# Per-token adapter with LayerNorm on one core: start of the kernel reordered, additions of b2 moved from VectorE to GpSimd and TensorE

## The chip, the core and the metric

The kernel runs on one core of a Trainium2 chip. The core has five engines, each with its own instruction stream: TensorE (PE; its weight loads are listed as PEld), VectorE (DVE), ScalarE (ACT), GpSimd (POOL) and SyncE (SP, which here only issues DMAs). They meet through semaphores. The metric is device time in microseconds (us); lower is better. The profile gives, for one execution, the span from the first to the last instruction.

## The reference

Every batch entry b has 128 tokens of 512 values, and a language id that chooses one of 10 small adapters:

```
w1, w2 = W1[id], W2[id]                    # 512x128 and 128x512
h       = relu(x @ w1 + b1[id])
y       = x + h @ w2 + b2[id]
normed  = (y - mean(y)) * rsqrt(var(y) + 1e-5)
out     = x + normed * gamma[id] + beta[id]
```

x is 128 x 128 x 512 in float32, all weights are float32; b1, b2, gamma and beta are small random rows, ten of each. Everything is read from and written to HBM once: 43.85 MB read, 33.55 MB written.

## The kernel before, in words

One batch entry (128 tokens on the 128 partitions, 512 columns) is the unit of work, and "b" counts them, 0 to 127. x comes in groups of four entries (`load_x`, four buffers, pool `xp`), results go out in pairs (`store`, tile `o`, five buffers, pool `op`, so pair g uses the buffer of pair g-5 once that pair's store has landed). For each entry:

- PE transposes x in four blocks (`transpose_x`, L235), ACT copies the result from PSUM (`copy_xT`, L239), PE multiplies by w1 (`down`, L258), ACT applies bias and relu (`relu`, L266), PE multiplies by w2 into a PSUM tile `y` of a pool of five (`up`, L275). ACT also copies the chosen w1 out of a resident table (`stage_w1`, L226).
- b2 is added in one of three ways. By default POOL makes r = x + b2 ahead of time (`add_b2`, L245, tile `r`, four buffers) and the residual reads r in place of x. For entries chosen by `b2_by_vector`, DVE adds b2 to y in PSUM (`vector_b2`, L285). For those of `b2_by_matmul`, PE adds a one-row product to y (`up`, L274).
- DVE adds the residual and sums the rows (`residual`, L292), ACT squares and sums (`square`, L315) and takes a reciprocal root (L325), DVE refines it (L329 to L334), multiplies by gamma (`scale`, L358) and writes the result on top of o (`finish`, L367). o was filled beforehand by POOL with x + beta (`add_beta`, L252).

The order on every engine is the order of the text, held by `keep()`, which chains each instruction to the one before it on its engine. The loop variable is i; entry i is transposed, entry i-1 goes through `down`, entry i-2 through `up`, and b = i-3 through the residual. POOL is told to do `add_b2(b + 2)` and then `add_beta(b)`: r is made two entries ahead of the loop's b, o at b itself. That is an order, not a time: POOL starts each as soon as its inputs and its buffer are there.

All loads and nearly all stores go through the SP queue in the order of the text: x (0,1), w2 of three languages, w1 of single entries (`load_first`, L154), x in halves of a group (`load_part`, L89), the rest of w2, two halves of a table of w1 (`load_early`, L162), then inside the loop x groups (L71), stores (L371) and, at i = 8, 10, 12 and 14, four quarters of a second table of w1 (`load_w1`, L103).

At the start, the thirty rows of beta, gamma and b2 (tile `rows`) must be spread over all partitions. DVE cuts them into three bf16 parts (L184 to L188, tile `parts`), PE multiplies a selecting column by the parts (`spread`, L206) and ACT or DVE copies each row out of PSUM (L209, L211), beta first, then gamma, then b2. Before that, PE runs ten matmuls on constants (`spin`). The first four entries' transposes and `down`s are mixed into the spreads.

At the end (b from 123 on) POOL does, in its order: the last r, the last four additions of beta, then for entries 123 and 124 the multiplication by gamma and the addition to o (`by_pool`, L415 and L417), and a quarter of entry 125. ACT issues the stores of 124 and 125 (`store_last`, L420), SP those of 126 and 127.

Of the kernel before, what the change touches and what calls it, by code (L numbers as in the profile page):

```python
# [22 lines left out]
U = 2  # L23
# [3 lines left out]
def cond_resid_kernel(ctx: ExitStack, tc: tile.TileContext, x, itok, W1, b1, W2, b2, gamma, beta, out):  # L27
# [8 lines left out]
    nc = tc.nc  # L36
    B, S, H = x.shape
    L, _, A = W1.shape
# [28 lines left out]
    E = B - 5  # L67
# [6 lines left out]
    def xb(b):  # L74
        return xs[b // G][:, b % G, :]
# [3 lines left out]
    rows = rp.tile([P, H], FP, tag="r", name="rows")  # L79
# [7 lines left out]
    def load_part(lo, hi):  # L87
        dst = xs[lo // G][:, lo % G : lo % G + hi - lo, :]
        keep(nc.sync.dma_start(out=dst, in_=x[lo:hi].rearrange("b s h -> s b h")))  # L89

    keep(nc.sync.dma_start(out=ids, in_=itok.rearrange("(o b) -> o b", o=1)))
    keep(nc.scalar.dma_start(out=rows[0:L, :], in_=beta))
    keep(nc.sync.dma_start(out=rows[L : 2 * L, :], in_=gamma))
    keep(nc.scalar.dma_start(out=rows[2 * L : 3 * L, :], in_=b2))
    load_part(0, 2)
    keep(nc.scalar.dma_start(out=b1r, in_=b1))

    warm = const.tile([P, 1], FP, name="warm")
# [2 lines left out]
    def load_w1(k):  # L101
        keep(
            nc.sync.dma_start(out=w1[:, :, k, :], in_=W1[:, k * P : (k + 1) * P, :].rearrange("l p a -> p l a"))  # L103
        )

    ident = const.tile([P, P], FP, name="ident")
    make_identity(nc, ident)
    eps = const.tile([P, 1], FP, name="eps")
    nc.gpsimd.memset(eps, EPS)
    ones = const.tile([P, P], BF, name="ones")  # L110
    nc.gpsimd.memset(ones, 1.0)

    R = 3 * L
    parts = const.tile([P, H], BF, name="parts")
# [16 lines left out]
    def lid(b, engine):  # L133
        g = b // G
        if (g, engine) not in lids:
            loads, vals = nc.values_load_multi_w_load_instructions(  # L136
                lang[0:1, g * G : (g + 1) * G],
                engines=[engine],
                min_val=0,
                max_val=L - 1,  # L140
                skip_runtime_bounds_check_because="clamped on the chip to 0..L-1 above",
            )
            for ins in loads:
                keep(ins)
            lids[g, engine] = vals
        return lids[g, engine][b % G]
# [33 lines left out]
    load_early(5, L)  # L180
    load_part(2 * G + 2, 3 * G)

    left = rp.tile([P, H], FP, tag="r", name="left")
    keep(nc.vector.tensor_copy(parts[0:R, :], rows[0:R, :]))  # L184
    keep(nc.vector.tensor_tensor(left[32 : 32 + R, :], rows[0:R, :], parts[0:R, :], ALU.subtract))
    keep(nc.vector.tensor_copy(parts[32 : 32 + R, :], left[32 : 32 + R, :]))
    keep(nc.vector.tensor_tensor(left[64 : 64 + R, :], left[32 : 32 + R, :], parts[32 : 32 + R, :], ALU.subtract))
    keep(nc.vector.tensor_copy(parts[64 : 64 + R, :], left[64 : 64 + R, :]))  # L188

    b1T = const.tile([P, L], FP, name="b1T")  # L190

# [23 lines left out]


    def b2_by_matmul(b):
        return b in (5, B - 1)

    def b2_by_vector(b):  # L220
        return b < 4 or 8 <= b < B - 8 and (b % 4 == 1 if b < 24 else b % 16 in (1, 6, 11) or b % 32 == 30)

    def stage_w1(b):
        w1s[b] = wp.tile([P, KC, A], FP, tag="w1s", name=f"w1s_{b}")
# [12 lines left out]
    def copy_xT(b):  # L237
        xT[b] = tp.tile([P, KC, P], FP, tag="xT", name=f"xT_{b}")
        keep(nc.scalar.copy(xT[b], pxs.pop(b)))  # L239

    def add_b2(b):
        if not b2_by_matmul(b) and not b2_by_vector(b):
            rs[b] = rp.tile([P, H], FP, tag="r", name=f"r_{b}")
            v = lid(b, ET.Pool)
            keep(nc.gpsimd.tensor_tensor(rs[b], xb(b), b2_b[:, bass.ds(v * H, H)], ALU.add))  # L245

    def add_beta(b):
        g, j = divmod(b, 2)
        if j == 0:
            os[g] = op.tile([P, 2, H], FP, tag="o", name=f"o_{g}")  # L250
        v = lid(b, ET.Pool)
        keep(nc.gpsimd.tensor_tensor(os[g][:, j, :], xb(b), beta_b[:, bass.ds(v * H, H)], ALU.add))  # L252

    def down(b):
        phs[b] = p_h.tile([P, P], FP, tag="h", name=f"ph_{b}")
        for k in range(KC):
            keep(
                nc.tensor.matmul(  # L258
                    phs[b], lhsT=w1s[b][:, k, :], rhs=xT[b][:, k, :], start=(k == 0), stop=(k == KC - 1)
                )  # L260
            )
        del xT[b], w1s[b]
# [217 lines left out]
    def spin(n, width):  # L480
        idle = p_s.tile([P, H], FP, tag="s", name="idle")
        for _ in range(n):
            keep(
                nc.tensor.matmul(
                    idle[:, :width], lhsT=ones, rhs=ones[:, 0:1].to_broadcast([P, width]), start=True, stop=True
                )
            )


    spin(9, H)  # L490
    spin(1, H // 2)

    def spread_turn(lo, hi):
        for r in range(lo, hi):
            spread(r, nc.scalar if r % 7 in (1, 3, 5) else nc.vector)

    def x_turn(b):
        transpose_x(b)
        copy_xT(b)

    x_turn(0)
    transpose_b1()
    spread_turn(0, 4)
    x_turn(1)
    spread_turn(4, 11)
    down(0)
    relu(0)
    spread_turn(11, 15)
    down(1)
    relu(1)  # L510
    x_turn(2)
    spread_turn(15, 19)
    x_turn(3)
    down(2)
    relu(2)
    spread_turn(19, 24)
    down(3)
    relu(3)
    spread_turn(24, R)
    up(0)  # L520
    up(1)

    for i in range(3, B + U):
        b = i - U - 1
        if b > G and b % G == 2 and b // G + 3 < NG:
            load_x(b // G + 3)
        if i == 5:
            load_x(3)
        if i in (8, 10, 12, 14):
            load_w1((i - 8) // 2)  # L530
        if i == 4:
            up(2)
        if i == 5:
            up(3)
        if i > 3 and on(i):
            transpose_x(i)
        if b <= E:
            add_b2(b + 2)
            add_beta(b)
        if i > 4 and on(i - 1):  # L540
            down(i - 1)
        if i > 3 and on(i):
            copy_xT(i)
        if b == 2:
            scalar_means(0)
            deviation(0)
        if i > 4 and on(i - 1):
            relu(i - 1)
        if i + 1 >= LATE and on(i + 1):
            stage_w1(i + 1)  # L550
        if i > 5 and on(i - U):
            up(i - U)


        g, half = divmod(b, 2)
        p = g - 1
        mine, old = 0 <= p < B // 2, 0 <= p - 1 < B // 2
        if b == E:
            add_b2(b + 3)
            add_beta(b + 1)  # L560
            add_b2(b + 4)
            for n in range(b + 2, B):
                add_beta(n)
        if b > E:
            tail(b)
        elif half == 0:
            if on(b):
                vector_b2(b)
                residual(b)
                square(b)  # L570
            if mine:
                scale(2 * p)
                rstd(p, 1)
            if old:
                finish(2 * p - 1)
                store(p - 1)
        else:
            if on(b):
                vector_b2(b)
            if mine:  # L580
                rstd(p, 2)
            if on(b):
                residual(b)
                square(b)
            if mine:
                rstd(p, 3)
                scale(2 * p + 1)
            if mine:
                finish(2 * p)
        if 0 < g and b <= E and half == 1:  # L590
            scalar_means(g)
            deviation(g)
        if FIRST <= i + 1 < LATE:
            stage_w1(i + 1)

        for n, engine in ((i + 3, ET.Activation), (i - U + 3, ET.PE), (b + 1, ET.DVE), (b + 5, ET.Pool)):
            if on(n):
                lid(n, engine)

# [36 lines left out]
```

## Time and profile before

| what | value |
|---|---|
| time, median of 3 runs | 308.75 us (308.27 to 308.82) |
| span of the profiled execution | 306.5 us (the page gives no other time of it) |
| granted TensorE clock, mean | 0.989 |
| busy: PE / DVE / ACT / POOL | 294.6 / 295.9 / 282.3 / 283.9 us |
| `add_beta` (L252), `add_b2` (L245) on POOL | 128 and 97 instructions |
| `vector_b2` (L285) on DVE | 29 instructions, 695 ns each |
| moved by DMA | 77.85 MB |

How to read it: a row of the timeline is start, duration, engine, line, operation, tiles and count, and in brackets how long the engine was idle before it and what ended the idle time. Spans of POOL instructions overlap their neighbours, so the distance from one start to the next, not the duration, is what an instruction costs. In the list of waits the three numbers are the total, the count and the longest, in us. The windows table gives busy time per engine in a stretch, then the granted clock, the DMA engines' busy share and the rate in GB/s.

### The profile page before, as it was taken

Reading aid. Unit: us, or ns where it says so; the run is one execution under the profiler, and the core shown is the slowest. Engines: PE = TensorE matmul, PEld = TensorE weight load, DVE = VectorE, ACT = ScalarE, POOL = GpSimd, SP = SyncE. Lnnn points to the kernel's source line nnn. Section 1 sums busy time; section 2 is a strip of 40 time slices with the busy share of each in tenths; the row PEclk is TensorE's granted clock in tenths of the full one; section 3 lists DMA queues with packets and bytes.
Section 4 is the critical chain, followed back from the end, with each engine's and each line's share of the span. In section 5 each row is a group of like instructions: output and inputs, shape, how many; then the busy total and the mean of one; then the engine's idle time right before and its main releaser. Section 6 shows DMA issues by size and latency. Waiting matters only on the chain. (4 is left out here: it accounts for less than half of the span.)

```text
span 306.5 us, 6981 instructions
## 1 busy us (share of the span) xinstructions
PE 294.6 (96%) x1835; PEld 220.0 (72%) x1835; DVE 295.9 (97%) x771; ACT 282.3 (92%) x777; POOL 283.9 (93%) x238
## 2 busy tenths in 40 slices
PE   8999999999999999999999999999999999999960
PEld 3748787777777777777777777777777777777730
DVE  6889999999999999999999999999999999999985
ACT  3858999999999999999999999999999999999981
POOL 1349899999999999999999999999999999999994
PEclk9999999999999999999999999999999999999995
DMA  6999999976678766766777666767776666773324
GB/s 231 379 390 388 373 371 354 387 231 240 221 255 276 250 202 241 226 257 219 259 276 243 213 209 238 265 224 260 275 238 206 226 231 242 246 266 137 135 109 171
DMA packets 43769, 77.85 MB, mean 254 GB/s; under 512 B 1961, under 2 KB 7348, under 8 KB 43730
## 3 DMA queue, kind: packets, MB, share of 16 engines
q1 hardware_dynamic: 43382, 76.84, 72.1%
q10 hardware_dynamic: 348, 0.57, 0.5%
q8 instruction: 15, 0.25, 0.3%
q14 instruction: 24, 0.20, 0.2%
HBM read 43.85 MB, written 33.55 MB: 253 GB/s over the span
## 5 line engine op out<-in xcount | busy, mean ns | idle before, releaser
L252 POOL TENSOR_TENSOR o<-x,beta_b 128x512 f32<-128x512 f32 x128 | 173.9, 1395 | 10.2 <-DVE beta_b L211 9.5
L245 POOL TENSOR_TENSOR r<-x,b_b 128x512 f32<-128x512 f32 x97 | 135.7, 1399 | 7.3 <-DVE b_b L211 6.2
L258 PE MATMUL ph<-xT,w1s 128*128 128x128 f32 x1024 | 135.4, 275 | 0.0
L275 PE MATMUL py<-w,hT 128*128 x256 | 131.2, 595 | 0.5 <-DVE b_b L211 0.5
L258 PEld LDWEIGHTS ph<-xT,w1s 128*128 128x128 f32 x1024 | 124.9, 192 | 1.0 <-ACT hT L266 0.5
L235 PEld LDWEIGHTS pxT<-ident,x 128*128 128x128 f32 x512 | 66.6, 151 | 65.3 <-issue 49.2
L358 DVE SCALAR_TENSOR_TENSOR py<-py,nmean,gamma_b 128x512 f32<-128x512 f32 x126 | 95.0, 754 | 0.9 <-ACT sq L399 0.8
L367 DVE SCALAR_TENSOR_TENSOR o<-py,rstd,o 128x512 f32<-128x512 f32 x122 | 91.2, 748 | 0.0
L315 ACT ACTIVATE sq<-py,sum 128x512 f32<-128x512 f32 x124 | 85.9, 693 | 2.8 <-DVE py L292 2.5
L235 PE MATMUL pxT<-ident,x 128*128 128x128 f32 x512 | 78.2, 276 | 0.0
L239 ACT COPY xT<-pxT 128x512 f32<-128x512 f32 x128 | 74.7, 584 | 3.5 <-PE pxT L235 3.5
L292 DVE SCALAR_TENSOR_TENSOR py<-py,r 128x512 f32<-128x512 f32 x97 | 67.0, 691 | 0.2
L226 ACT COPY w1s<-w 128x512 f32 x107 | 65.5, 612 | 0.0
L266 ACT ACTIVATE hT<-ph,b1T 128x128 f32<-128x128 f32 x128 | 46.9, 366 | 7.9 <-PE ph L258 2.6
L275 PEld LDWEIGHTS py<-w,hT 128*128 128x128 f32 x256 | 39.1, 192 | 2.9 <-issue 1.0
L315 ACT ACTIVATION_READ_ACCUMULATOR sq<-py,sum 128x1 f32 x124 | 25.0, 202 | 0.0
L292 DVE SCALAR_TENSOR_TENSOR py<-py,x 128x512 f32<-128x512 f32 x31 | 21.7, 699 | 0.4
L285 DVE TENSOR_TENSOR py<-py,b_b 128x512 f32<-128x512 f32 x29 | 20.2, 695 | 0.7 <-PE py L275 0.6
L325 ACT ACTIVATE root<-ssq,eps 128x2 f32<-128x2 f32 x62 | 16.4, 265 | 0.0
L292 DVE DVE_READ_ACCUMULATOR py<-py,r 128x1 f32 x97 | 13.7, 141 | 0.0
L306 ACT ACTIVATE nmean<-sum 128x2 f32<-128x2 f32 x62 | 12.3, 198 | 0.0
L329 DVE SCALAR_TENSOR_TENSOR part<-ssq,root 128x2 f32<-128x2 f32 x62 | 9.3, 151 | 0.2 <-ACT root L325 0.2
(55 smaller groups left out, 90.4 us busy)
## 6 DMA issues: line engine op xcount, KB each, us to landing
out_dram<-o SPq DMA_DIRECT2D x61, 512.0 KB, 3.4
x<-in_x_dram SPq DMA_DIRECT2D x29, 1024.0 KB, 6.2
x<-in_x_dram SPq DMA_DIRECT2D x6, 512.0 KB, 8.8
w1e<-in_L_cond_W_dram SPq DMA_DIRECT2D x2, 1280.0 KB, 12.3
w<-in_L_cond_W_dram SPq DMA_DIRECT2D x4, 640.0 KB, 8.1
w1s<-in_L_cond_W_dram SPq DMA_DIRECT2D x9, 256.0 KB, 8.4
w<-in_L_cond_W_dram SPq DMA_DIRECT2D x1, 1792.0 KB, 10.3
w<-in_L_cond_W_dram SPq DMA_DIRECT2D x1, 768.0 KB, 5.4
```

Source lines behind the costliest of these rows:

```text
L226: keep(nc.scalar.copy(w1s[b].rearrange("p k a -> p (k a)"), src))
L235: keep(nc.tensor.transpose(pxs[b][:, k, :], cols, ident))
L239: keep(nc.scalar.copy(xT[b], pxs.pop(b)))
L245: keep(nc.gpsimd.tensor_tensor(rs[b], xb(b), b2_b[:, bass.ds(v * H, H)], ALU.add))
L252: keep(nc.gpsimd.tensor_tensor(os[g][:, j, :], xb(b), beta_b[:, bass.ds(v * H, H)], ALU.add))
L258: nc.tensor.matmul(phs[b], lhsT=w1s[b][:, k, :], rhs=xT[b][:, k, :], start=(k == 0), stop=(k == KC - 1))
L266: keep(nc.scalar.activation(hT[b], phs.pop(b), AF.Relu, bias=b1T[:, bass.ds(lid(b, ET.Activation), 1)]))
L275: keep(nc.tensor.matmul(ys[b], lhsT=hT[b], rhs=w2[:, bass.ds(v * H, H)], start=not m, stop=True))
L292: nc.vector.scalar_tensor_tensor(ys[b], ys[b], 1.0, r, ALU.mult, ALU.add, accum_out=col(sums, b))
L315: nc.scalar.activation(sq, ys[b], AF.Square, bias=col(sums, b), scale=-float(H), accum_out=col(ssqs, b))
L358: nc.vector.scalar_tensor_tensor(ys[b], ys[b], col(nmeans, b), gamma_b[:, bass.ds(v * H, H)], ALU.add, ALU.mult)
L367: nc.vector.scalar_tensor_tensor(o, ys.pop(b), rstds[g][:, j : j + 1], o, ALU.mult, ALU.add)
```

## The change

- The load of x for entry 0 is issued alone, followed by entry 1; gamma's ten rows are loaded through ACT's queue, between beta and b2, and no longer through SP's.
- The bf16 parts of the thirty rows: the upper half of each float32 word, read as bf16, is the first part. DVE subtracts it from the rows (into partitions 32 on), ACT copies it; the same again gives the second part, and the second subtraction writes the third part. Three casts of DVE become two copies of ACT.
- `spin` runs six matmuls of 512 columns in place of nine and a half; the constant `ones` is set before the identity.
- `add_beta` of entries 0 to 3 comes before every `add_b2`; in the loop it is done for b + 2, beside `add_b2(b + 2)`, instead of for b.
- b2 of entries 0, 2, 30, 62 and 94 goes from DVE to POOL; b2 of 1 and 3 goes from DVE to PE.
- In the start, the turns of spreads, transposes and `down`s are cut differently, and POOL's register loads of the ids are asked for one entry earlier.

```
-    load_part(0, 2)
+    load_part(0, 1)
+    load_part(1, 2)
...
-    keep(nc.vector.tensor_copy(parts[0:R, :], rows[0:R, :]))
-    keep(nc.vector.tensor_tensor(left[32 : 32 + R, :], rows[0:R, :], parts[0:R, :], ALU.subtract))
-    keep(nc.vector.tensor_copy(parts[32 : 32 + R, :], left[32 : 32 + R, :]))
-    keep(nc.vector.tensor_tensor(left[64 : 64 + R, :], left[32 : 32 + R, :], parts[32 : 32 + R, :], ALU.subtract))
-    keep(nc.vector.tensor_copy(parts[64 : 64 + R, :], left[64 : 64 + R, :]))
+    def upper(lo):
+        return rows[lo : lo + R, :].bitcast(BF)[:, 1 : 2 * H : 2]
+    keep(nc.vector.tensor_tensor(rows[32 : 32 + R, :], rows[0:R, :], upper(0), ALU.subtract))
+    keep(nc.scalar.copy(parts[0:R, :], upper(0)))
+    keep(nc.vector.tensor_tensor(parts[64 : 64 + R, :], rows[32 : 32 + R, :], upper(32), ALU.subtract))
+    keep(nc.scalar.copy(parts[32 : 32 + R, :], upper(32)))
...
     def b2_by_matmul(b):
-        return b in (5, B - 1)
+        return b in (1, 3, 5, B - 1)
     def b2_by_vector(b):
-        return b < 4 or 8 <= b < B - 8 and (b % 4 == 1 if b < 24 else b % 16 in (1, 6, 11) or b % 32 == 30)
+        return 8 <= b < B - 8 and (b % 4 == 1 if b < 24 else b % 16 in (1, 6, 11))
...
-    spin(9, H)
-    spin(1, H // 2)
+    spin(6, H)
...
-    spread_turn(0, 4)
+    spread_turn(0, 5)
     x_turn(1)
-    spread_turn(4, 11)
+    spread_turn(5, 11)
+    for n in range(4):
+        add_beta(n)
     down(0)
...
     spread_turn(11, 15)
+    x_turn(2)
     down(1)
     relu(1)
-    x_turn(2)
-    spread_turn(15, 19)
+    spread_turn(15, 20)
...
-    spread_turn(24, R)
+    spread_turn(25, R)
+    add_b2(0)
     up(0)
     up(1)
...
             add_b2(b + 2)
-            add_beta(b)
+            if 4 <= b + 2 <= E:
+                add_beta(b + 2)
```

More of the change, by code (lines that the diff above doesn't have):

```diff
@@ L92, in cond_resid_kernel @@
     keep(nc.scalar.dma_start(out=rows[0:L, :], in_=beta))
-    keep(nc.sync.dma_start(out=rows[L : 2 * L, :], in_=gamma))
+    keep(nc.scalar.dma_start(out=rows[L : 2 * L, :], in_=gamma))
     keep(nc.scalar.dma_start(out=rows[2 * L : 3 * L, :], in_=b2))
-    load_part(0, 2)
+    load_part(0, 1)
+    load_part(1, 2)
     keep(nc.scalar.dma_start(out=b1r, in_=b1))
@@ L104, in load_w1 @@
         )
+    ones = const.tile([P, P], BF, name="ones")
+    nc.gpsimd.memset(ones, 1.0)
     ident = const.tile([P, P], FP, name="ident")
@@ L109, in cond_resid_kernel @@
     nc.gpsimd.memset(eps, EPS)
-    ones = const.tile([P, P], BF, name="ones")
-    nc.gpsimd.memset(ones, 1.0)
     R = 3 * L
@@ L181, in cond_resid_kernel @@
     load_part(2 * G + 2, 3 * G)
-    left = rp.tile([P, H], FP, tag="r", name="left")
-    keep(nc.vector.tensor_copy(parts[0:R, :], rows[0:R, :]))
-    keep(nc.vector.tensor_tensor(left[32 : 32 + R, :], rows[0:R, :], parts[0:R, :], ALU.subtract))
-    keep(nc.vector.tensor_copy(parts[32 : 32 + R, :], left[32 : 32 + R, :]))
-    keep(nc.vector.tensor_tensor(left[64 : 64 + R, :], left[32 : 32 + R, :], parts[32 : 32 + R, :], ALU.subtract))
-    keep(nc.vector.tensor_copy(parts[64 : 64 + R, :], left[64 : 64 + R, :]))
+    def upper(lo):
[4 more added lines that the diff above has]
+    keep(nc.scalar.copy(parts[32 : 32 + R, :], upper(32)))
     b1T = const.tile([P, L], FP, name="b1T")
@@ L515, in cond_resid_kernel @@
     relu(2)
-    spread_turn(19, 24)
+    spread_turn(20, 25)
     down(3)
     relu(3)
-    spread_turn(24, R)
+    spread_turn(25, R)
+    add_b2(0)
     up(0)
@@ L594, in cond_resid_kernel @@
             stage_w1(i + 1)
-        for n, engine in ((i + 3, ET.Activation), (i - U + 3, ET.PE), (b + 1, ET.DVE), (b + 5, ET.Pool)):
+        for n, engine in ((i + 3, ET.Activation), (i - U + 3, ET.PE), (b + 1, ET.DVE), (b + 6, ET.Pool)):
             if on(n):
```

## The prediction

> **What bounds the kernel now.** I read the page first, then the table by stretches, the list of waits, the timeline of POOL, the landing of one store and the chain that ended last.
>
> ```profile
> span 306.5 us, 6981 instructions
> PE 294.6 (96%) x1835; PEld 220.0 (72%) x1835; DVE 295.9 (97%) x771; ACT 282.3 (92%) x777; POOL 283.9 (93%) x238
> ...
> DMA  6999999976678766766777666767776666773324
> ```
> ```profile
> 7.00:20.00 13.00, 12.54 (x76) 8.55 (x75) 10.72 (x17) 9.93 (x21) 2.83 (x3) 1.00 1.03 384
> 20.00:33.00 13.00, 13.00 (x79) 9.79 (x78) 12.63 (x32) 10.07 (x29) 12.03 (x10) 1.00 1.05 386
> 33.00:60.00 27.00, 27.00 (x171) 21.04 (x171) 26.86 (x70) 26.13 (x74) 26.18 (x22) 1.00 1.07 371
> 60.00:290.00 230.00, 230.00 (x1470) 174.71 (x1469) 229.64 (x602) 225.37 (x629) 230.00 (x187) 1.00 0.68 233
> ```
>
> Past 60 us PE, DVE and POOL have no free time: three engines are balanced. Up to 60 us the DMA engines are also full, at 371 to 386 GB/s, and POOL has 10.2 us free before 20 us and 1.8 later.
>
> The shares don't say which one leads, so I lined up the starts by entry. A PE round takes 2.19 us (2.22 for entries under 21). DVE needs 2.06 us an entry and 0.69 more for one whose b2 it adds; it trails `up` by 0.1 to 1.25 us and has held PE up three times by 0.15 us (transposes of 38, 70 and 102), behind the crowded additions at 30, 62 and 94. POOL makes an instruction every 1.232 us (52.43 to 291.43 us, 194 steps) and is 4 to 7.5 us early with r, 3.9 for entry 126.
>
> ```profile
> POOL r L245 <- DMA x<-in_x_dram: 1.1, 1, 1.1
> ...
> POOL o L252 <- DMA out_dram<-o: 0.5, 1, 0.5
> ```
> ```profile
> 41.80 1.29 POOL L245 TENSOR_TENSOR r<-x,b_b 128x512 f32<-128x512 f32 x1
> 43.19 1.27 POOL L252 TENSOR_TENSOR o<-x,beta_b 128x512 f32<-128x512 f32 x1
> ...
> 50.59 1.30 POOL L245 TENSOR_TENSOR r<-x,b_b 128x512 f32<-128x512 f32 x1
> 52.43 1.27 POOL L252 TENSOR_TENSOR o<-x,beta_b 128x512 f32<-128x512 f32 x1 [0.54 <-DMA out_dram<-o]
> ```
> ```profile
> L371 SPq DMA_DIRECT2D out_dram<-o x1: 1718/1718/1718, 34.2 to 34.2; - x1
> ...
> DMA to landing us min/median/max: 8.9/8.9/8.9
> ```
>
> POOL's two waits after 20 us lie in the stretch where the DMA engines are full. By the order of POOL's instructions, the one at 43.19 is o of entry 12 and the one at 52.43 o of entry 16. Each needs the o buffer five pairs back, so store 1 (issued 34.18, landed 8.9 us later, at 43.1) and store 3 (which ends the wait of 0.54). Start against start, 43.19 is 1.39 after 41.80, 0.16 more than the usual 1.23: a small wait as well. Stores land late because x and w1 are queued ahead of them.
>
> ```profile
> 291.65 4.91 POOL o L252 x4
> 296.56 1.22 POOL n L415
> 297.79 0.04 issue
> 297.83 0.05 POOLq L415
> 297.87 1.25 POOL o L417
> 299.13 1.23 POOL n L415
> 300.36 0.07 issue
> 300.43 1.27 POOL o L417
> ```
>
> The chain's last 50 us are POOL without a break. ACT had n of entry 123 ready at 294.90 (L413 in the timeline), and POOL took it up at 296.56 (by this chain): the last four additions of beta were in the way. POOL ends at 302.10, DVE at 303.04; DVE's last store, issued 303.10, lands 2.3 us later and the span ends 1.1 after that. POOL's own last store (ACT, issue 302.21) takes 2.0 to 2.5 by the neighbours: POOL's end has some 0.7 us to spare, no more.
>
> **The change, part by part.** The sum is against the span of 306.5; the median of 308.75 lies 2.25 above it, and I carry that over.
>
> *Start.* Three and a half fewer spins of 0.43 us: 1.5. x of entry 0 is issued 0.35 earlier (in gamma's place on SP) and half as long (262 KB at 384 GB/s, 0.7); the pair landed at 5.1, so it comes near 4.0. Two issues of 0.4 replace gamma's 0.3 and one of 0.4, so w2 behind them moves by 0.1. The parts took DVE 3.13 to 5.88 (casts 0.41, 0.42, 0.42, subtractions 0.68 twice); now two subtractions, with ACT's copies (0.61 by L226) beside them: 1.4, so 1.35 shorter. Against it, b2's rows go third in ACT's queue (0.3 later), behind an x that is now issued before them; landing 1.7 us after issue, as now, gives a gain of 1.0; 3.6 after issue, as the x of 1.51 took, a loss of 0.9. I take a gain of 1.0 to 1.3 at `up(0)`; the rows are tiny like the ones that land today. Two more b2 matmuls of 0.22 for entries 1 and 3 lie in rounds where PE waits for ACT anyway; if it didn't, 0.4. Four b2 additions of 0.70 leave DVE, but residual 0 must now wait for POOL's r (1.3 after the last b2 row), so about 0.5 is left of the 2.8.
>
> *What is late next.* x of entries 10 and 11 lands 14.0 us after 19.06, at 33.03, and PE transposes 10 at 33.80. The DMA engines are full, so that landing moves by the 0.35 of the first issue. PE's whole start gain is cut to about 1.1 there. The three late b2 additions give back the three holds of 0.15: 0.45. PE and DVE alone would end 1.5 earlier.
>
> *POOL.* It does 102 additions of b2 instead of 97: 0 and 2, and 30, 62, 94. Additions 0 and 2, with beta 0 to 3, fall before the x of entry 10, for which it waits today. On the face of it POOL is then two betas ahead, 2.46 us, and pays three instructions, 3.70: 1.2 behind.
>
> But beta two entries earlier asks for the o buffers two entries earlier, and those come with the stores. POOL can't start o of 12 before store 1 lands: 43.1, less 0.35. Before that instruction it had by then made r of 14; in the new order it has only made r of 12. Seven instructions (o 12, o 13, r 14, o 14, r 15, o 15, r 16) take it to 51.4, and o of 16 waits for store 3 again, at 52.4 less 0.35. Before it had r up to 18 done at that point; now up to 16 (17 is DVE's). So the head start is gone, and one instruction more remains to be done: r of 18, 30, 62 and 94, 4 x 1.232 = 4.93, less 0.35, is 4.6. From here POOL has no free time in which to catch up. The bounds of the 0.35 are 0 (the stream is no earlier) and 0.95 (store 3 lands before POOL is there).
>
> *End.* All that POOL does after o of 16 is 4.6 later: its last instruction ends near 306.7 in place of 302.1. r of 124 comes at 293.7, and DVE used it at 291.16, so DVE ends 2.6 later at 305.7, not last. ACT issues POOL's last store at 306.8, it lands 2.0 to 2.5 later, and 1.1 follow: span 309.9 to 310.4, 3.7 over 306.5. The time is 308.75 + 3.7 = 312.4; with the bounds 311.6 to 313.2.
>
> The Trainium skill, page "GPSIMD Engine Reference", section "4.1 Engine selection", advises against an elementwise two-input addition on GpSimd, as about twice as slow as VectorE. In these rows it is 1.232 against 0.695, 1.8 times. At twice, the four would cost 5.56 and the time would be 313.0; the rows decide.
>
> **The rivals.**
>
> *The stores don't hold POOL* (ends on the other side). If stores 1 and 3 landed before POOL asks, near 41 and 49, the head start stays and POOL's old waits of 0.7 go too: its end is 3.70 - 2.46 - 0.7 - 0.35 = 0.2 later, 302.3 (the 0.35 is the earlier x of entry 10), where POOL's end has 0.7 to spare. DVE ends 1.5 earlier, and the span is about 306.0, the time 308.2. It decides where store 1 lands 2 us earlier. For it: SP issues stores up to 1 us earlier if DVE is earlier. Against: 8.9 us from issue to landing with the engines full, so that what is ahead sets the landing. The Trainium skill, "DMA: Bandwidth & Descriptors", section "Queues, rings and completion order", says descriptors are taken in ring order on each engine, but that completion is not first in, first out for an issuing engine; by the second half a store might overtake, and the time would be this rival's. The rows speak for the first half: the store of 34.18 took 8.9, the load of 19.06 took 14.0.
>
> *Half of it:* store 1 or 3 is earlier by about 1.2 us, one instruction is saved, 311.2 and down to 310.0.
>
> *More than it:* rows landing late, or DVE and PE, once r is just in time (near entry 37, when today's lead of 5 to 6 less 3.4 of order and 1.1 to 1.7 of PE's advance is gone), lose more at the end: one or two of DVE's tail steps behind r of 124 to 126, up to 315.
>
> **How the numbers follow.** POOL held as worked out (311.5 to 313.4): 0.75. Half: 0.09. More: 0.06. Not held: 0.10, around 308.2, with 307.7 to 308.8. A time of this kernel can be told from no change at 0.2%, 0.6 us. Faster by more than that (under 308.15) is 0.07 and within it 0.04, which is the case "not held" and 0.01 of "half"; slower is 0.89. The range 310.0 to 313.9 leaves out the rival of the other side, and a little above. Its centre is 312.4.
>
> **What would show it.** The waits list of the new kernel should have POOL's `add_beta` waiting for stores about 4 us in all, o of 10 among them, instead of 0.5; o of 16 should start within 0.4 of 52.1; POOL should be full from there on, and DVE's residual should wait for r, in small pieces past some 100 us, 3 to 4 us in total, with PE idle as much. Beta 0 to 3 should stand before the first r. Transpose 10 should be about 1 us earlier, POOL's last instruction near 306.7. The prediction is wrong if POOL's wait for stores stays under 1 us, or if POOL has r 5 us early at entry 100.

## The result, and the profile after

The changed kernel takes 313.38 us (median of 4 executions, 312.76 to 314.69); the kernel before, beside it, 308.53 (4 executions, 308.27 to 308.82). The ratio is 1.016, with a 95% interval of 1.0135 to 1.0186: slower by 4.85 us. The forecast was 312.4, with a range of 310.0 to 313.9.

The profiled execution of the new kernel is the slowest of its four, 314.69 us at a span of 312.9; the other spans are 311.0 to 311.9. The time lies 1.8 above the span in each of these executions.

The page of the new kernel opens with these lines (busy us, share of the span, instructions):

```profile
span 312.9 us, 6991 instructions
...
PE 298.3 (95%) x1833; PEld 221.7 (71%) x1833; DVE 291.6 (93%) x761; ACT 284.2 (91%) x779; POOL 289.9 (93%) x243
```

DVE is 4.3 us less busy and POOL 6.0 us more. The table by stretches shows where each is still free (PE, PEld, DVE, ACT, POOL busy; then granted clock, DMA share, GB/s):

```profile
7.00:20.00 13.00, 13.00 (x70) 9.08 (x69) 8.91 (x14) 8.87 (x18) 4.96 (x4) 1.00 1.05 390
20.00:33.00 13.00, 12.95 (x70) 8.83 (x68) 9.98 (x27) 9.06 (x25) 10.92 (x9) 1.00 1.04 383
33.00:60.00 27.00, 27.00 (x173) 21.33 (x172) 26.56 (x67) 25.86 (x73) 23.92 (x21) 1.00 1.04 339
60.00:290.00 230.00, 229.54 (x1458) 173.76 (x1457) 226.71 (x592) 223.92 (x624) 230.00 (x187) 1.00 0.69 234
```

From 33 to 60 us POOL has 3.1 us free where it had 0.8; past 60 us it alone has no gap, while DVE's busy time there falls from 229.64 to 226.71. PE ran 70 matmuls from 7 to 20 us, where it ran 76 before, although it shows no idle time. The list of waits names POOL's free time and DVE's:

```profile
DVE py L295 <- POOL r L248: 3.9, 9, 1.4
POOL o L255 <- DMA out_dram<-o: 3.1, 3, 1.7
...
DVE rows L188 <- DMA rows<-in_L_cond_b_dram: 1.9, 1, 1.9
```

The timeline of POOL gives the three waits for stores (start, duration, and in brackets the idle time before and its releaser):

```profile
41.77 1.29 POOL L248 TENSOR_TENSOR r<-x,b_b 128x512 f32<-128x512 f32 x1
43.64 2.50 POOL L255 TENSOR_TENSOR o<-x,beta_b 128x512 f32<-128x512 f32 x2 [0.57 <-DMA out_dram<-o]
46.10 1.28 POOL L248 TENSOR_TENSOR r<-x,b_b 128x512 f32<-128x512 f32 x1
48.17 1.27 POOL L255 TENSOR_TENSOR o<-x,beta_b 128x512 f32<-128x512 f32 x1 [0.80 <-DMA out_dram<-o]
...
51.86 1.28 POOL L248 TENSOR_TENSOR r<-x,b_b 128x512 f32<-128x512 f32 x1
54.86 2.52 POOL L255 TENSOR_TENSOR o<-x,beta_b 128x512 f32<-128x512 f32 x2 [1.71 <-DMA out_dram<-o]
```

By POOL's order, 43.64 is o of entry 12 and 54.86 o of entry 16; the r at 51.86 is that of entry 16. At this point POOL used to have r up to 18. The store that ends the last wait is store 3, issued at 46.0 (L374, stretch 45.5 to 46.5):

```profile
L374 SPq DMA_DIRECT2D out_dram<-o x1: 1107/1107/1107, 46.0 to 46.0; - x1
...
DMA to landing us min/median/max: 8.8/8.8/8.8
```

It lands at 54.8, 2.4 later than before. The chain that ended last has the same shape, later (start, us):

```profile
295.05 3.93 POOL r L248 x3
298.98 4.90 POOL o L255 x4
303.88 1.23 POOL n L418
305.19 1.25 POOL o L420
306.44 1.22 POOL n L418
```

The start did not go as forecast either. The timeline of PE:

```profile
1.01 2.74 PE L487 MATMUL idle<-ones 128*128 128x512 bf16 x6 [1.01 <-POOL ones L108]
4.20 1.10 PE L238 MATMUL pxT<-ident,x 128*128 128x128 f32 x4 [0.45 <-DMA x<-in_x_dram]
...
6.16 2.31 PE L209 MATMUL row<-parts,pick 96*128 96x512 bf16 x5 [0.65 <-DVE parts L190]
...
9.12 2.76 PE L209 MATMUL row<-parts,pick 96*128 96x512 bf16 x6
...
12.98 1.03 PE L209 MATMUL row<-parts,pick 96*128 96x512 bf16 x4
```

Five spreads take 2.31 us and six 2.76; the four at 12.98 take 1.03. The starts of neighbouring spreads are 0.43 apart in the first two groups and 0.22 in the last. The change lies between 11.3 and 13.0 us; up to there these matmuls ran at half the later rate, and inside a group no idle time shows it. `up` of entry 0 ends at 21.95 (20.04 before), and transpose 10 starts at 36.31 (33.80 before).

### The profile page after: what moved, and what is told of

Read it like the earlier page. It is cut to its first block, busy times and chain, and to the rows that moved or that the text cites. A ratio compares the mean times of both kernels' runs of the same rounds, so it can differ in the third digit from the quotient of the medians.

```text
span 312.9 us, 6991 instructions
## 1 busy us (share of the span) xinstructions
PE 298.3 (95%) x1833; PEld 221.7 (71%) x1833; DVE 291.6 (93%) x761; ACT 284.2 (91%) x779; POOL 289.9 (93%) x243
## 4 chain that ended last, share of the span: by engine, by line
POOL 35%; PE 31%; issue 15%; DVE 13%; POOLq 2%; DMA 1%; ACT 1%; ACTq 0%; DVEq 0%
POOL o L255 20%; POOL r L248 13%; PE ph L261 12%; PE py L278 10%; PE pxT L238 6%; DVE py L361 4%; DVE py L295 4%; DVE o L370 3%; PE row L209 3%; DMA rows<-in_L_cond_b_dram 1%; DVE py L288 1%; POOL n L418 1%; DVE b_b L214 1%; POOLq L248 1%; POOL o L420 1%
## 5 line engine op out<-in xcount | busy, mean ns | idle before, releaser
L248 POOL TENSOR_TENSOR r<-x,b_b 128x512 f32<-128x512 f32 x102 | 142.1, 1398 | 4.8 <-DVE b_b L214 4.8
L295 DVE SCALAR_TENSOR_TENSOR py<-py,r 128x512 f32<-128x512 f32 x102 | 70.9, 695 | 5.6 <-POOL r L248 3.9
L295 DVE SCALAR_TENSOR_TENSOR py<-py,x 128x512 f32<-128x512 f32 x26 | 18.2, 700 | 0.2
L288 DVE TENSOR_TENSOR py<-py,b_b 128x512 f32<-128x512 f32 x22 | 15.2, 693 | 0.1
L295 DVE DVE_READ_ACCUMULATOR py<-py,r 128x1 f32 x102 | 14.6, 143 | 0.0
L209 PE MATMUL row<-parts,pick 96*128 96x512 bf16 x30 | 9.8, 470 | 0.7 <-DVE parts L190 0.7
```

The source lines that it names most:

```text
L295: nc.vector.scalar_tensor_tensor(ys[b], ys[b], 1.0, r, ALU.mult, ALU.add, accum_out=col(sums, b))
```

## The experiments

All are edits of the new kernel except where "before" is said. All times are medians; the kernel before took 308.63, 308.58 and 308.70 in the three groups of runs. The line numbers move by one or two between kernels, so tiles tell more than lines.

### The spin of before in the new kernel

```
-    spin(6, H)
+    spin(9, H)
+    spin(1, H // 2)
```

> The changed kernel with the spin of before (nine and a half matmuls on constants instead of six), all else as changed. In the changed kernel the thirty spread matmuls start at 6.16 us (6.58 before) but then follow each other by 0.43 us up to 11.3, where before it was 0.22 to 0.26, and the first product with w2 comes at 20.85 instead of 18.94. Theory 1 (the shorter spin leaves PE at half rate until 12.6 us): full rate from about 6.4 us, first product with w2 near 18.5, store 3 landed near 52.4, o of entry 16 near 52.4 instead of 54.86, and POOL and the end 2.4 earlier: 311.0 us. Theory 2 (the late landing of the rows of b2, 4.6 instead of 3.0 us, makes the late start): the spin changes nothing, first product with w2 stays near 20.9, time stays near 313.4 us.

Measured: 314.33 (313.75 to 314.71), ratio 1.0189 [1.0164, 1.0213]. The spreads are fast again (timeline of PE), and `up` of entry 0 ends at 19.55, 2.4 us earlier. The end did not follow: POOL (second fence, its timeline) again starts o of 12 and o of 16 on a store.

```profile
6.14 1.25 PE L209 MATMUL row<-parts,pick 96*128 96x512 bf16 x5
```

```profile
38.20 1.28 POOL L255 TENSOR_TENSOR o<-x,beta_b 128x512 f32<-128x512 f32 x1 [2.49 <-DVE py L361]
...
44.23 2.50 POOL L255 TENSOR_TENSOR o<-x,beta_b 128x512 f32<-128x512 f32 x2 [1.06 <-DMA out_dram<-o]
...
54.20 2.52 POOL L255 TENSOR_TENSOR o<-x,beta_b 128x512 f32<-128x512 f32 x2 [1.28 <-DMA out_dram<-o]
```

The first row is o of 10. Its wait is listed under another releaser, but it needs the buffer of pair 0, and store 0 lands at 38.06, so this too is a wait for a store. A start 2.4 us earlier moved o of 16 by only 0.66. What POOL pays for is the landing of store 3, and here that is late although the start is not: the first w2 landed at 8.49 us (7.06 in the new kernel's profile), and x of entries 10 and 11 at 34.11 (32.89). The fast start of theory 1 came true; neither expected time was met.

### The three late additions back on DVE

```
-        return 8 <= b < B - 8 and (b % 4 == 1 if b < 24 else b % 16 in (1, 6, 11))
+        return 8 <= b < B - 8 and (b % 4 == 1 if b < 24 else b % 16 in (1, 6, 11) or b % 32 == 30)
```

> The changed kernel with b2 of entries 30, 62 and 94 back on VectorE. Theory 1 (POOL is the bound and each instruction it has more after o of entry 16 costs 1.23 us at the end): POOL ends 3.7 earlier; that alone would give 309.7, but PE and DVE, which transpose entry 10 2.5 us later than before, then end last: 311.0 us, with no waits of DVE for r after 30 us. Theory 2 (the late start is all of the loss): the three additions are free on POOL, time stays near 313.4 or rises by 0.4.

Measured: 310.53 (309.66 to 311.94), ratio 1.0069 [1.0047, 1.0091]: 2.85 us less than the new kernel, against three instructions of 1.232 (3.70). POOL's last instruction ends at 305.09, 4.3 earlier than in the profile above. After the start, r is nowhere so late that DVE waits for it. The timeline of POOL ends with

```profile
303.42 1.68 POOL L420 TENSOR_TENSOR o<-n,o 128x512 f32<-128x512 f32 x2
```

The half-rate start is in this profile too (five spreads in 2.32 us), and here it counts: `up` of entry 0 ends at 22.32, 2.3 later than in the kernel before, and DVE, no longer held by POOL, ends at 305.91, 2.9 later.

### Six buffers for o

Room for the sixth is made by one buffer less for hT and a single one for sq.

```
-    op = ctx.enter_context(tc.tile_pool(name="op", bufs=5))
+    op = ctx.enter_context(tc.tile_pool(name="op", bufs=6))
...
-        hT[b] = tp.tile([P, P], FP, tag="hT", name=f"hT_{b}", bufs=6)
+        hT[b] = tp.tile([P, P], FP, tag="hT", name=f"hT_{b}", bufs=5)
...
-        sq = tp.tile([P, H], FP, tag="sq", name=f"sq_{b}")
+        sq = tp.tile([P, H], FP, tag="sq", name=f"sq_{b}", bufs=1)
```

> The changed kernel with six o buffers instead of five (the room comes from one sq buffer instead of two and five hT buffers instead of six). Theory 1 (doing beta two entries earlier makes POOL wait for stores, and the time is lost for good): o of 12, 14 and 16 now wait for the store one earlier; POOL's waits for stores fall from 3.1 us to under 0.3, o of 16 starts near 51.6 instead of 54.86, POOL ends 3.3 earlier, and the end is that of the late PE and DVE or of POOL, whichever is later: 310.5 us, 310.0 to 311.0. Theory 2 (POOL would have had to wait anyway, for x or for r buffers): waits of another name take their place and the time stays within 0.5 of 313.4.

Measured: 311.92 (311.52 to 312.27), ratio 1.0114 [1.0092, 1.0136]. o of 16 now starts at 49.42, 5.4 earlier, and o of 12 at 40.70, neither waiting. The wait has moved to the next instruction that needs the buffer of pair 3, o of 18 (timeline of POOL):

```profile
55.30 1.27 POOL L255 TENSOR_TENSOR o<-x,beta_b 128x512 f32<-128x512 f32 x1 [2.13 <-DMA out_dram<-o]
```

One wait of 2.1 in place of three of 3.1 in all: a buffer more gains 1.5, not the 2.9 expected, because store 3 still lands near 55. (The start is a fast one in this profile, with `up` of entry 0 ending at 19.56; against the run with the long spin, whose start is fast too, the gain is 2.4.) That the waits come from the o buffers is shown; that one more buffer ends them is refuted.

### The short spin in the kernel before

```
-    spin(9, H)
-    spin(1, H // 2)
+    spin(6, H)
```

> The kernel before with the shorter spin of six matmuls as its only edit. Theory 1 (the spin decides when PE gets to full rate): the spread matmuls from about 6.4 us on follow each other by 0.43 us until about 12 us, the first product with w2 comes 1.5 to 2 us later than 18.94, and the time rises by as much, since PE, DVE and POOL have nothing to make it up with: 310.3 us (309.5 to 311). Theory 2 (the spin is only idle filling): PE starts on x as it lands at 5.07, the time stays within 0.3 of 308.5.

Measured: 310.40 (309.39 to 310.93), ratio 1.0056 [1.0029, 1.0083], as expected. The timeline of PE has the half rate in the old kernel too:

```profile
6.32 1.89 PE L206 MATMUL row<-parts,pick 96*128 96x512 bf16 x4
...
8.86 3.17 PE L206 MATMUL row<-parts,pick 96*128 96x512 bf16 x7
```

Transpose 10 starts at 36.16 in place of 33.80. By itself the short spin costs 1.8 us.

### Beta back at b in the loop

```
-            if 4 <= b + 2 <= E:
-                add_beta(b + 2)
+            if 4 <= b:
+                add_beta(b)
```

> The changed kernel with beta back at b in the loop (beta of entries 0 to 3 still ahead of everything, from entry 4 on beta of b beside b2 of b + 2, as before). Theory 1 (asking for the o buffers two entries earlier is what makes POOL wait for stores, and it costs one instruction's place in POOL's order and the stretch of those waits): POOL's waits for stores fall from 3.1 us to about 0.5, POOL ends 1 to 3 earlier, time 311.6 us (310.8 to 312.4). Theory 2 (the three late additions and the start are the whole loss, the order is indifferent): 313.4.

Measured: 312.72 (311.99 to 313.22), ratio 1.0139 [1.0122, 1.0156]. The median is 0.66 below the new kernel's, of the 1.23 that one instruction less would give, but the intervals of the two ratios overlap, so the times alone don't show a gain. In its profile r of 18 is made before o of 16, as in the kernel before, and POOL waits 1.4 us for stores in 2 waits:

```profile
53.39 1.28 POOL L255 TENSOR_TENSOR o<-x,beta_b 128x512 f32<-128x512 f32 x1 [1.15 <-DMA out_dram<-o]
```

POOL ends at 306.74 there and at 309.41 in the new kernel's profile: one instruction, and 1.47 by which o of 16 starts earlier. (These are the fastest of four executions here and the slowest of four there.) The expected gain was too large; the median lies above the expected range.

### The three late additions on POOL in the kernel before

```
-        return b < 4 or 8 <= b < B - 8 and (b % 4 == 1 if b < 24 else b % 16 in (1, 6, 11) or b % 32 == 30)
+        return b < 4 or 8 <= b < B - 8 and (b % 4 == 1 if b < 24 else b % 16 in (1, 6, 11))
```

> The kernel before with b2 of entries 30, 62 and 94 moved from VectorE to GpSimd as its only edit. Theory 1 (POOL is full from 60 us on and the chain at the end runs through it, so that an instruction more is 1.23 us later at the end, less the 0.7 that POOL's end has to spare): 3.7 - 0.7 = 3.0, 311.6 us; DVE hardly waits for r, as r of 126 comes 3.9 early today. Theory 2 (the 4 to 7 us by which r is early are slack and take up the 3.7): three holds of PE by 0.15 go, 308.2 us.

Measured: 311.54 (310.94 to 311.70), ratio 1.0089 [1.0072, 1.0105], as expected. Nothing waits for r but once, at the end (list of waits), yet the end is 3 us later, as the timeline of POOL shows:

```profile
DVE py L292 <- POOL r L245: 0.4, 1, 0.4
```

```profile
295.84 4.98 POOL L252 TENSOR_TENSOR o<-x,beta_b 128x512 f32<-128x512 f32 x4
...
304.69 1.67 POOL L417 TENSOR_TENSOR o<-n,o 128x512 f32<-128x512 f32 x2
```

POOL ends at 306.36 in place of 302.10. The lead of 4 us that r had all through the kernel before was not slack: POOL's last instructions come after the same stream, whatever r's lead.

### The start's spin and gamma's queue back

```
-    keep(nc.scalar.dma_start(out=rows[L : 2 * L, :], in_=gamma))
+    keep(nc.sync.dma_start(out=rows[L : 2 * L, :], in_=gamma))
...
-    spin(6, H)
+    spin(9, H)
+    spin(1, H // 2)
```

> The changed kernel with the long spin and with gamma's rows again on SP's queue ahead of x: of the start's edits only the split of x and the parts in fewer steps are left, the rest is as changed. Theory 1 (POOL is held by the stores 1 and 3, and from there on by its own work, whatever the start does): the rows land near 3.1 us, the first product with w2 comes near 17.7, earlier than before and 3 earlier than in the changed kernel, and still o of 16 starts only when store 3 lands, at 52.0 to 54.2, so that the time stays at 312.3 to 314.3 us. Theory 2 (the late start is the larger part of the loss): about 3 less than the changed kernel, 310.4.

Measured: 313.50 (312.14 to 314.29), ratio 1.0147 [1.0115, 1.0179], as expected: no gain, although `up` of entry 0 ends at 19.20, 2.75 us earlier than in the new kernel. o of 16 starts at 54.17, when store 3 has landed (timeline of POOL):

```profile
54.17 2.51 POOL L255 TENSOR_TENSOR o<-x,beta_b 128x512 f32<-128x512 f32 x2 [1.34 <-DMA out_dram<-o]
```

### Start, late additions and order of beta back

To the edit before are added those of the second and the fifth experiment. What stays of the change is the split load of x, the shorter way to the parts, beta of 0 to 3 first, and b2 of 0 to 3 on POOL and PE.

> The long spin, gamma on SP ahead of x, beta at b in the loop from entry 4 on, and b2 of 30, 62 and 94 on VectorE; left of the change are the split of x, the parts in fewer steps, beta of 0 to 3 ahead, and b2 of 0 to 3 on GpSimd and TensorE. Theory 1: POOL has five instructions more in its idle time before 33 us and none later, PE and DVE start 1 us earlier and keep what the landing of x of 10 and 11 leaves of it: 307.6 us (307.0 to 308.4). Theory 2 (POOL's order at the start alone costs, since r of 0 has to be waited for): 308.6 or more.

Measured: 309.83 (309.26 to 310.06), ratio 1.004 [1.0027, 1.0053]; expected was less than the kernel before. In its profile the first w2 lands at 9.08 (7.35 before) and x of entries 10 and 11 at 34.11 (33.03 before). The only difference left among the loads was x of batch 0 on its own, which leads to the next two.

### As the last, with x of entries 0 and 1 in one load

```
-    load_part(0, 1)
-    load_part(1, 2)
+    load_part(0, 2)
```

> The run with the long spin, gamma on SP, beta at b and 30, 62 and 94 on VectorE (309.83 us), with x of entries 0 and 1 loaded by one DMA again. Where x was loaded by two, the slowest DMA engine brought the first part of w2 at 8.2 to 9.1 us (7.06 in one profile), where it was loaded by one at 7.2 to 7.35, and all later landings kept the lag. Theory 1 (the split of x costs that lag): w2 lands near 7.3, x of 10 and 11 near 33.0 instead of 34.1, PE transposes entry 10 at 33.1 instead of 34.5, 308.4 us (307.8 to 308.9). Theory 2 (the lag comes from something else): time stays at 309.8.

Measured: 308.63 (307.86 to 308.92, 11 executions), ratio 0.9994 [0.9984, 1.0003], as expected. The split load cost 1.2 us. POOL's order at the start is the same in the two runs, so it was not the cause of the loss. What is left of the change is worth nothing that can be told: transpose 10 starts 0.5 earlier, at 33.28, capped by x of entries 10 and 11, which lands at 33.03 again.

### The split load alone, in the kernel before

The same edit the other way round.

> The kernel before with x of entries 0 and 1 loaded by two DMAs as its only edit. Theory 1 (the split costs a lag of the slowest DMA engine of about 1 us in all that lands up to 60 us): x of 10 and 11 lands near 34.1, stores 1 and 3 near 44.1 and 53.4, PE is held at entry 10 by about 0.4 and POOL by 1: 309.3 us (308.9 to 309.8). Theory 2 (two DMAs in place of one change nothing but the first landing): 308.6.

Measured: 309.75 (308.89 to 310.33, 9 executions), ratio 1.0027 [1.0016, 1.0038]: a loss of 1.05. The list of DMAs issued up to 4 us (tile, count, KB, median us from issue to landing) of this kernel,

```profile
w<-in_L_cond_W_dram SPq DMA_DIRECT2D x1, 768.0 KB, 7.1
x<-in_x_dram SPq DMA_DIRECT2D x2, 256.0 KB, 2.9
```

and of the kernel before:

```profile
w<-in_L_cond_W_dram SPq DMA_DIRECT2D x1, 768.0 KB, 5.4
x<-in_x_dram SPq DMA_DIRECT2D x1, 512.0 KB, 3.6
```

The halves of x themselves come sooner, w2 behind them is issued 0.42 later and lands another 1.7 later. From 2 to 8 us the tables by stretches give 232 GB/s here and 315 before:

```profile
2.00:8.00 6.00, 5.94 (x25) 2.96 (x24) 4.86 (x13) 3.24 (x6) 0.00 (x0) 1.00 0.85 232
```

```profile
2.00:8.00 6.00, 5.94 (x23) 2.96 (x22) 4.51 (x12) 2.85 (x5) 0.00 (x0) 1.00 0.88 315
```

### POOL's edits alone

Spin, gamma and the load of x as before; order of beta and b2 as in the new kernel.

```
-    keep(nc.scalar.dma_start(out=rows[L : 2 * L, :], in_=gamma))
+    keep(nc.sync.dma_start(out=rows[L : 2 * L, :], in_=gamma))
...
-    load_part(0, 1)
-    load_part(1, 2)
+    load_part(0, 2)
...
-    spin(6, H)
+    spin(9, H)
+    spin(1, H // 2)
```

> The changed kernel with the long spin, gamma on SP and x of 0 and 1 by one DMA: of the start only the parts in fewer steps are left, and all of POOL's edits (beta two entries ahead, 102 additions of b2). This is what the forecast took for granted of the start. Theory 1: store 1 lands near 43.1, store 3 near 52.4, o of 16 starts then with r up to 16 done, POOL has four instructions more than before from there on, 4.93 less 0.7 to spare: 312.6 us (312.2 to 313.0). Theory 2 (the loss beyond 3.0 us came from the start): with that gone it is the 311.5 of the kernel before with three more additions on GpSimd.

Measured: 313.09 (312.54 to 313.58), ratio 1.0144 [1.0128, 1.0159]: 4.4 us over the kernel before, with an undisturbed start (transpose 10 at 33.63). The median is 0.1 above the expected range. The waits and the timeline of POOL are close to those of the forecast, which had o of 16 at 52.1 and waits for stores of about 4 us:

```profile
DVE py L294 <- POOL r L247: 4.4, 12, 1.4
...
POOL o L254 <- DMA out_dram<-o: 3.5, 3, 1.7
```

```profile
43.17 2.51 POOL L254 TENSOR_TENSOR o<-x,beta_b 128x512 f32<-128x512 f32 x2 [1.07 <-DMA out_dram<-o]
...
52.62 2.51 POOL L254 TENSOR_TENSOR o<-x,beta_b 128x512 f32<-128x512 f32 x2 [0.76 <-DMA out_dram<-o]
```

### An attempt at a better kernel

Start as before, x in one load, six buffers for o (with the edits that make room), beta at b + 2, b2 of 0 to 3 all on PE, 30 and 62 on POOL, 94 on DVE.

```
-        return b in (1, 3, 5, B - 1)
+        return b in (0, 1, 2, 3, 5, B - 1)
...
-        return 8 <= b < B - 8 and (b % 4 == 1 if b < 24 else b % 16 in (1, 6, 11))
+        return 8 <= b < B - 8 and (b % 4 == 1 if b < 24 else b % 16 in (1, 6, 11) or b == 94)
```

> An attempt at a better kernel: long spin, gamma on SP, x of 0 and 1 by one DMA, six o buffers with beta two entries ahead, b2 of 0 to 3 on TensorE, of 30 and 62 on GpSimd and of 94 on VectorE. Theory 1 (with six buffers the head start of two betas is kept, and pays for two of the late additions): POOL waits for stores under 0.7 us and is at o of 18 when store 3 lands, two instructions ahead of before; PE loses only one hold of 0.15 and the start gives up to 0.7: 307.9 us (307.4 to 308.6). Theory 2 (the sixth buffer only moves the wait on to store 3, and the additions cost as before): 310 or more.

Measured: 308.58 (307.90 to 308.96, 11 executions), ratio 0.9993 [0.9984, 1.0002]. POOL waits 0.7 for stores in all, at o of 18 (timeline of POOL):

```profile
52.57 1.27 POOL L254 TENSOR_TENSOR o<-x,beta_b 128x512 f32<-128x512 f32 x1 [0.69 <-DMA out_dram<-o]
```

The head start pays for two more additions: POOL ends at 302.40 (302.10 before). DVE ends at 302.69 (303.04 before), and the time is that of the kernel before.

## One sum that covers the runs

If store 3 pins o of 16 and POOL has no gap afterwards, POOL's end is that of the kernel before (302.10), plus what o of 16 starts later than 52.43, plus 1.232 for each instruction that has come to stand behind o of 16. From the timelines:

| kernel profiled | o of 16 starts | instructions more behind it | end worked out | POOL's end measured |
|---|---|---|---|---|
| changed kernel | 54.86 | 4 (r of 18, 30, 62, 94) | 309.46 | 309.41 |
| spin of before | 54.20 | 4 | 308.80 | 308.86 |
| spin and gamma of before | 54.17 | 4 | 308.77 | 308.70 |
| POOL's edits alone | 52.62 | 4 | 307.22 | 307.17 |
| beta back at b | 53.39 | 3 (30, 62, 94) | 306.76 | 306.74 |
| before, three on POOL | 53.09 | 3 | 306.46 | 306.36 |
| three back on DVE | 54.22 | 1 (r of 18) | 305.12 | 305.09 |
| before, split load | 54.82 | 0 | 304.49 | 304.47 |
| start, late additions and order of beta back | 54.13 | 0 | 303.80 | 303.72 |
| the same, x of 0 and 1 in one load | 52.73 | 0 | 302.40 | 302.40 |

The two ends agree within 0.1 in every row. With six buffers the pin is o of 18, here in the kernel before:

```profile
57.37 2.52 POOL L252 TENSOR_TENSOR o<-x,beta_b 128x512 f32<-128x512 f32 x2
```

In the changed kernel with six buffers it starts at 55.30, with five instructions more behind it (r of 19 and 20 too), which gives 306.19 against 306.17 measured. The old kernel with the short spin is the one with five buffers that is not so close: 303.16 worked out, 303.77 measured, of which 0.3 is a wait of POOL for DVE to free a buffer of r. In the six kernels of the table whose POOL ends at 306.3 or later the span ends 3.5 to 3.6 after POOL; in the others it ends 3.9 to 4.3 after it; in these DVE ends within 0.9 us of POOL, so that POOL alone doesn't set the end.

This is also why the losses don't add. The short spin costs 1.8 by itself, the split load 1.05 and POOL's edits 4.4, 7.25 together; the change costs 4.85. While POOL is last, a late start counts only by what it moves the landing of store 3.

## Why the prediction was right, and which terms were off

**POOL held by stores: right.** o of 12 and o of 16 wait for stores 1 and 3, r stands at 16 when o of 16 begins, four instructions more are left, and POOL is full from there. All of it is in the profile of the changed kernel and, with spin, gamma and the load of x as before, in that of POOL's edits alone. POOL's end in the latter is 307.17, forecast 306.7; the waits for stores are 3.5 us there and 3.1 in the changed kernel, forecast about 4. o of 10 was named among the waiting; it waits in POOL's edits alone, but not in the changed kernel, where POOL comes to it at 38.08; there o of 14 waits.

**The landings: mis-sized.** The step "at 52.4 less 0.35", with bounds of 0 and 0.95 earlier, took it that the stream of transfers can only be as late as before or earlier. Store 3 landed 2.4 later in the changed kernel's profile and 1.0 to 2.9 later in the others that load x apart. o of 16 starts 2.8 later than the 52.1 of the forecast, and that is the whole excess of the profiled span over it: it ends 6.4 later, forecast 3.7. (The upper bound of 313.2 comes out as 313.0 from the terms shown.)

In the changed kernel's profile the loads up to 33 us were not late: x of entries 10 and 11 landed at 32.89, against 33.03 before. What was late is what SP issues in its order from the first store on. Store 0 left at 32.09 in place of 30.11, because its results came later (`finish` of entry 1 ends at 32.06 in place of 30.08), and the loads behind it had to wait for it. From 36 to 40 us the DMA engines then moved 261 GB/s in place of 368 (tables by stretches, changed kernel and kernel before):

```profile
36.00:40.00 4.00, 4.00 (x29) 3.29 (x28) 3.81 (x10) 3.85 (x12) 4.00 (x4) 1.00 0.99 261
```

```profile
36.00:40.00 4.00, 4.00 (x28) 3.30 (x27) 3.87 (x12) 3.85 (x12) 4.00 (x4) 1.00 1.09 368
```

In this execution, then, the late start moved the stores, and not a lag of the split load. The kernel before with the short spin shows the same (store 0 at 32.46, 293 GB/s), but there store 3 landed only 1.1 later; where the rest of the 2.4 comes from is open.

**The start: wrong sign.** The step was "I take a gain of 1.0 to 1.3 at `up(0)`", and the profile shows a loss of 1.9. Two things failed. Rows of b2 issued third in ACT's queue landed about 3 us after their issue (DVE's first subtraction starts at 4.70 after an idle of 1.91), nearer to the 3.6 that the text had and did not take than to the 1.7 that it took. And the shorter spin was costed as 1.5 us less of matmuls; with it the spreads ran at half rate until after 11.3 us. The short spin alone costs 1.8 in the old kernel. The runs tell the two apart, by one profile each: with the long spin `up` of entry 0 ends 2.4 earlier, at 19.55, and with gamma's queue back as well another 0.35 earlier, at 19.20. So the half rate is the larger part by far, and what was left out is a cost of the spin that its length doesn't show. With neither, `up` of entry 0 ends 0.8 earlier than before, of the 1.0 to 1.3 forecast. The cap on PE's gain at transpose 10 was right in mechanism, and is seen where x is whole (33.28 against a landing of 33.03), but the changed kernel never came there: its transpose 10 is 2.5 later, not 1 earlier.

**The price of the split load: not in the sum.** It was put down as a half that lands sooner and 0.1 more for w2. It costs 1.05 in the old kernel and 1.2 in the eighth experiment against the ninth.

**What carried over: off by 0.45.** The 2.25 between median and span was taken from a median and a profile that was one of the faster executions. Execution by execution the difference is 1.8.

**DVE waits for r: near in size, too early in time.** 3.9 us in 9 waits, 1.4 of it for r of entry 0; the 2.5 that come late stand against a forecast of 3 to 4 (3.0 in POOL's edits alone). In the changed kernel r comes just in time from entry 63 (its r starts at 158.3 us), not from entry 37 or 100 us: PE had not gained the 1.1 to 1.7 us that the text took from r's lead, it had lost. In POOL's edits alone, with the undisturbed start, it is entry 48, at 124 us.

**The rivals.** "The stores don't hold POOL" is refuted by three waits for stores, and "half" by the four instructions left behind o of 16, none of them saved. "More than it" named rows that land late and a tail behind r. The rows were late, but the sum above leaves nothing for DVE's tail. The median of 313.38 is within the 311.5 to 313.4 given for the main case, 0.98 over its centre. That it is so near is luck in part: in the profiled execution, the one that can be taken apart, the landings of stores put the sum too low by 2.7 and the 0.45 put it too high. That POOL's edits alone give 4.4 of the 4.85 is shown. The rest of 0.45 is less than the two intervals can tell from nothing (1.0128 to 1.0159 there, 1.0135 to 1.0186 for the change). What share the spin and the split load have in it isn't shown, since the two are hidden behind each other.

## What to carry to other kernels

An engine that makes things ahead of time isn't idle by its lead: where its last instructions end the kernel, an instruction moved onto it costs its full time, less what its end has to spare, however early its results are: here three of 1.232 us cost 3.0. Work moved earlier in an engine's order moves its demand for buffers earlier as well; before counting a head start, look up when the transfer that frees each buffer lands. With one buffer more the wait comes back at the next instruction that needs a buffer of the same late transfer. Shortening a warm-up or splitting a load at the start is to be costed by its effect on the rate of what follows, not by its own length.

## What the runs showed of the hardware

**PE has a half rate at the start that the granted clock row doesn't show.** Matmuls of 512 columns in bf16 follow each other by 0.43 us until a moment of change and by 0.22 after it; the windows give a granted clock of 1.00 in both. With the spin of nine and a half eight of nine profiled kernels were fast from the first spreads on, which start at 5.97 to 6.58 us; in the ninth, the kernel before with three additions on POOL, the first two steps from 6.62 on were 0.41 and 0.31, and 0.22 came after them. With six, four of five were slow until some 10 to 13 us (the changed kernel's, those with the short spin in the kernel before, with three additions back and with beta at b), and one, with six o buffers, was fast from 6.18 on: the timeline of PE there has

```profile
1.01 2.74 PE L487 MATMUL idle<-ones 128*128 128x512 bf16 x6 [1.01 <-POOL ones L108]
...
6.18 1.25 PE L209 MATMUL row<-parts,pick 96*128 96x512 bf16 x5 [0.87 <-DVE parts L190]
```

with the same spin of 2.74 us as in the changed kernel. The Trainium skill, "TensorE: Matmul & The Clock Gate", section "What's actually happening", describes a clock gate that lets the array run at half rate until it has been busy for a window of about 3.4 us, a window that runs freely and does not start with the kernel. The two steps, 0.43 and 0.22, agree with it, and so does it that the moment of change is no fixed time: a spin of 3.8 to 4.5 us sufficed in eight of nine profiles, one of 2.7 in one of five. The length of the window doesn't come out of the traces; in the run with start, late additions and order of beta back and x in one load, the change falls into the spin, 2.9 us after its first matmul. That the window's phase made the difference between the five was not tried.

**Splitting one load delayed the loads behind it.** In seven of the eight profiled kernels with x of entries 0 and 1 in two loads, the last of the 16 parts of the first w2 landed at 8.2 to 9.5 us, while the first landed at 6.5 to 7.0; in the eighth, the changed kernel's, the last came at 7.06. In all six kernels with one load it came at 7.19 to 7.37. The lag of some of the DMA engines stayed in the stream: x of entries 10 and 11 landed at 33.25 to 34.63 us in those seven, at 33.02 to 33.23 in the six, and at 32.89 in the changed kernel's. In the old kernel with the split load it was 34.63 in place of 33.03, and store 3 landed at about 54.8 in place of 52.4. What makes those engines late, and why the changed kernel's profile shows no lag, was not settled.
